# The second MLP product of a vision tower by seven quarter products instead of eight, with the sums on VectorE

## The chip, the cores and the metric

The kernel runs on one core of a Trainium2 chip. The core has TensorE (PE in the profile, with PEld for its weight loads), VectorE (DVE), ScalarE (ACT), GpSimd (POOL) and the DMA engines with their queues (SP issues most transfers here). The metric is the device time of one execution, in microseconds (us). All data is float32.

## The reference, cut to what matters

The input is cut into patches and embedded: 32 blocks of 512 tokens of width D = 256. Then comes one layer with a retention and an MLP, and then a mixture of 8 experts of which each token uses two.

```python
h = _L0_tok_ref(x, L0_tok_W)                       # patches, DFT, @ W.T
# --- retention and MLP, on layernorm(h) ---
q, k, v = h1 @ Wq.T + bq, h1 @ Wk.T + bk, h1 @ Wv.T + bv
mem = decay * mem + (k * v)_t;  ret_t = q_t * mem  # a scan over the tokens
x = x + ret
h2 = _layernorm(x, ln2_g, ln2_b)
mlp = jax.nn.relu(h2 @ W1.T + b1) @ W2.T + b2      # 256 -> 1024 -> 256
x = x + mlp
# --- mixture of experts, on layernorm(h) ---
logits = tokens @ router_w.T;  probs = softmax(logits); top 2, weights normalised
for e in range(8):
    y = gelu(tokens @ w1[e] + b1[e]) @ w2[e] + b2[e]
    out = out + combine[:, e:e + 1] * y
```

What is changed is the product `relu(...) @ W2.T`: for a block it is [512 tokens x 1024] times [1024 x 256].

## The kernel before

The main loop works on three blocks at once: `new` (block i: embedding and retention), `mid` (block i-1: MLP) and `old` (block i-2: routing). Between these parts stand `slot(known)` calls; each enters one expert tile of 256 tokens (`enter`, L799) and ends the one before (`leave`, L816, and `sums`, L833 and L835); this is 16 passes on TensorE. The order of the instructions on TensorE, VectorE, ScalarE and SP is the order of this code; each engine works through its own list. The numbers L... are line numbers of this kernel, as the profile shows them.

```python
p_mm = ...tile_pool(name="p_mm", bufs=4, space=PSUM)   # tiles "mm", 4 in turn
p_tm = ...tile_pool(name="p_tm", bufs=3, space=PSUM)   # tiles "tm", 3 in turn
p_sm = ...tile_pool(name="p_sm", bufs=1, space=PSUM)   # tile "sm", one only
...
for i in range(NS):                       # NS = 31; new, mid, old as above
    embed = new.embed(); next(embed)      # L353: 20 matmuls into three tm tiles
    if mid: mid.features2()               # hT for the MLP (L292 on ScalarE)
    if old: old.rows(); old.turn3(); old.store()     # L533: row <- tok
    next(embed); next(embed)              # L359: h of the new block, norms
    if mid: mid.sum_up()                  # L462, L463: h += z, h += b2
    next(embed, None)                     # L252: zz and z
    slot(known)
    if old: old.join3()                   # L292: tokT
    for m in range(KH):                   # KH = 8
        if mid: mid.mlp_in(m)             # L298 w1, ScalarE relu into aT (L482)
        if m == 1: new.split1()
        if m == TT - 1: slot(known)
        if m == KH - 3:
            blocks[i + 1].differences(xs.pop(i + 1))   # L330, L327
            new.features1()               # L292: hT for the retention
    if old:
        for t in range(TT): old.logits(t) # L557, into sm
    for m in range(KD):                   # KD = 2
        new.retention(m)                  # L298 wqkv; kv L418, scan L426, ret L436
        if old and m == 0: old.choose()   # L579 to L595: small sums on VectorE
    if old: take(old.i + 1, old, old.place())   # L624 into sm; L626 to L735; scatter L640
    slot(known)
    if mid: mid.mlp_out(0)                # L492, L499
    new.residual()                        # L451 transposes, L454, norm, L252 zz
    slot(known)
    ...
    new.split2()                          # zz to features2 of the next period, by DMA
    if mid: mid.mlp_out(1)                # L492, L499, norm, L252 tok
```

The part that changes:

```python
def mlp_in(self, m):
    if m == 0:
        self.aT = one.tile([P, KH, BLK], F32, name="aT")      # BLK = 512 tokens
    ps = feature_mm(w1_sb, self.hT, m)
    nc.scalar.activation(self.aT[:, m, :], ps, AF.Relu, bias=...)

def mlp_out(self, u, between=None):
    if u == 0:
        self.norm = Norm()
    ps = p_tm.tile([P, 2, D], F32, name="tm")
    for i in range(2):
        if i and between:
            between()
        for k in range(KH):
            nc.tensor.matmul(                                  # L492
                ps[:, i, :],
                lhsT=self.aT[:, k, ts(u * 2 + i, P)],          # the weights: 128 x 128 of aT
                rhs=w2_sb[:, k, :],                            # streamed: 128 x 256
                start=k == 0, stop=k == KH - 1,
            )
    nc.vector.tensor_tensor(self.h[:, ts(u, 2), :], ps, self.h[:, ts(u, 2), :], ALU.add)   # L499
    for i in range(2):
        self.norm.stats(self.h, u * 2 + i)                     # L223, L224
    if u == U - 1:
        self.norm.factors_here() if self.i >= NS - 1 else self.norm.factors()   # on POOL in the loop
        self.tok = one.tile([P, TT, D], F32, name="tok")
        self.norm.apply(self.tok, self.h)                      # L252
        ...
```

And three short pieces that the steps of the prediction use:

```python
def sums(self):                       # of an expert tile, on VectorE
    nc.vector.scalar_tensor_tensor(share, ...)                 # L828
    nc.vector.tensor_tensor(share, share, ...)                 # L831
    nc.vector.tensor_tensor(y, ps, w[...])                     # L833: reads the tile's tm
    for c in range(2):
        nc.vector.tensor_scalar(y[:, c, :], y[:, c, :], share[:, c : c + 1], None, ALU.mult)  # L835
    # then two indirect adds to out by DMA

def residual(self):
    for u in range(U):                # U = 2
        ps = p_tm.tile([P, 2, D], F32, name="tm")
        ...                           # L451: transposes of ret, 128 x 128
        nc.vector.tensor_tensor(self.z[...], ps, self.z[...], ALU.add)          # L454
        ...                           # L223, L224: statistics
    norm.factors_here()               # L231 to L237, VectorE
    norm.apply(self.zz, self.z)       # L252

# wu, once at the start, a sum of 256 elements a partition from SBUF to SBUF:
nc.vector.tensor_tensor(wu[:, 4, j, :], E_j, O_j, ALU.subtract)                 # L142
```

Of the kernel before, what the change touches and what calls it, by code (L numbers as in the profile page):

```python
# [12 lines left out]
F32 = mybir.dt.float32  # L13
I32 = mybir.dt.int32
U16 = mybir.dt.uint16
AF = mybir.ActivationFunctionType
ALU = mybir.AluOpType
AX = mybir.AxisListType

P = 128  # L20
# [15 lines left out]
def vit_tower_kernel(  # L36
# [15 lines left out]
    nc = tc.nc  # L52
    B, NBLK, _, XW = x.shape
    D = wtok.shape[2]
    C = P // 2
    H = w1.shape[1]
    E = rw.shape[1]
    KD, KH = D // P, H // P
    J = STRIDE // 2
    TT = 4  # L60
    BLK = TT * P
    U = TT // 2
# [8 lines left out]
    RW = D + 4  # L71
# [3 lines left out]
    NS = NB - 1  # L75
# [73 lines left out]
    nc.sync.dma_start(out=w1_sb, in_=w1.rearrange("(k p) h -> p k h", p=P))  # L149
    w2_sb = const.tile([P, KH, D], F32)  # L150
    nc.sync.dma_start(out=w2_sb, in_=w2.rearrange("(k p) d -> p k d", p=P))
    rw_sb = const.tile([P, KD, E], F32)
# [156 lines left out]
    class Block:  # L309
# [168 lines left out]
        def mlp_in(self, m):  # L478
# [3 lines left out]
            nc.scalar.activation(self.aT[:, m, :], ps, AF.Relu, bias=vec[:, MB1 + m : MB1 + m + 1])  # L482

        def mlp_out(self, u, between=None):
            if u == 0:
                self.norm = Norm()
            ps = p_tm.tile([P, 2, D], F32, name="tm")
            for i in range(2):
                if i and between:
                    between()  # L490
                for k in range(KH):
                    nc.tensor.matmul(  # L492
                        ps[:, i, :],
                        lhsT=self.aT[:, k, ts(u * 2 + i, P)],
                        rhs=w2_sb[:, k, :],
                        start=k == 0,
                        stop=k == KH - 1,
                    )
            nc.vector.tensor_tensor(self.h[:, ts(u, 2), :], ps, self.h[:, ts(u, 2), :], ALU.add)  # L499
            for i in range(2):  # L500
                self.norm.stats(self.h, u * 2 + i)
            if u == U - 1:
                self.norm.factors_here() if self.i >= NS - 1 else self.norm.factors()
                self.tok = one.tile([P, TT, D], F32, name="tok")
                self.norm.apply(self.tok, self.h)
                if self.i == NS:
                    nc.vector.tensor_tensor(self.h, self.h, self.tok, ALU.add)
                    return
                mean, rstd = self.norm.mv[:, :, 0], self.norm.rstd[:, 0, :]
                self.by = small.tile([P, 2, TT], F32, name="by")  # L510
                nc.vector.tensor_scalar(self.by[:, 0, :], rstd, 1.0, None, ALU.add)
                nc.vector.scalar_tensor_tensor(self.by[:, 1, :], mean, -1.0, rstd, ALU.mult, ALU.mult)

# [15 lines left out]
        def rows(self):  # L529

            self.row = two.tile([P, TT, RW], I32, name="row")
            for i, half in enumerate(halves(self.tok)):
                nc.scalar.copy(self.row.bitcast(U16)[:, :, i * D : (i + 1) * D], half)  # L533
            nc.gpsimd.iota(
                self.row[:, :, NUMBER : NUMBER + 1],
                pattern=[[1, TT]],
                base=self.i * BLK,
                channel_multiplier=TT,
            )
# [147 lines left out]
    def take(n, block, writes):  # L687
# [24 lines left out]
        shape = [1, k, E]  # L712
        past = small.tile([1, KMAX, E], F32, name="past")[:, :k, :]
        nc.vector.tensor_tensor(
# [4 lines left out]
        )  # L719
        table_f = small.tile([1, 2, KMAX], F32, name="table_f")[:, :, :k]  # L720
        nc.vector.tensor_reduce(table_f[:, 0, :], past, AX.X, ALU.add)
# [216 lines left out]
    def slot(known):  # L938

        if len(tiles) - at["enter"] > LEFT and at["enter"] + 2 <= known:  # L940
            expert_step()
# [7 lines left out]
    with tc.manual_schedule(engines=MANUAL):  # L949
        blocks[0].differences(xs.pop(0))  # L950
        xs[1] = load_x(1)
        for i in range(NS):
# [36 lines left out]
            if old:  # L989
                for t in range(TT):  # L990
                    old.logits(t)
            for m in range(KD):
                new.retention(m)
                if old and m == 0:
                    old.choose()
            if old:
                take(old.i + 1, old, old.place())
            if i + 2 < NB:
                xs[i + 2] = load_x(i + 2)
            slot(known)  # L1000
            if mid:
                mid.mlp_out(0)
            new.residual()
            slot(known)
            if at["enter"] == 0:

                advance("load", 2)
            if i == 0:
                fold(w1_sb.unsqueeze(1), G2, B2, MB1)
            else:  # L1010
                new.split2()
            if mid:
                mid.mlp_out(1)

# [27 lines left out]
        writes = old.place()  # L1042
        next(weights)
        last.retention(0)
        mid.mlp_out(0)
        next(weights)
        take(NS - 1, old, writes)
        expert_step()
        mid.mlp_out(1)
        next(weights)  # L1050
# [21 lines left out]
        for m in range(KH):  # L1072
            last.mlp_in(m)
            if m == TT - 1:
                expert_step()
        expert_step()
        last.mlp_out(0, expert_step)
        expert_step()
        last.mlp_out(1, expert_step)

# [103 lines left out]
```

## Time and profile before

| | |
|---|---|
| time, median of 3 runs | 2197.89 us (2197.12 to 2201.64) |
| span of the profiled execution | 2216.1 us |
| granted TensorE clock, mean | 0.991 |
| L492 (second MLP product), PE busy | 462.3 us, 2048 passes |
| L298 with w1 (first MLP product), PE busy | 455.4 us, 1024 passes |
| L298 with wqkv, PE busy | 342.5 us, 768 passes |
| L353 (embedding), PE busy | 284.8 us, 1280 passes |
| L499 (adding the product to h), DVE busy | 44.2 us, 64 times, 690 ns each |

The profile shows one execution. PE is the matmul row of TensorE and PEld its weight loads, which overlap it. The ends of matmuls are modelled; their starts are recorded. In a row of a group or of the timeline stand the line, the engine, the operation, the tiles written and read (out<-in), the shape (partitions x elements) and how many there are. In a group row the busy time and the mean duration follow; in the timeline the start in us comes first and then how long the row lasted; `[3.54 <-PE mm L298]` at its end is how long the engine stood idle before it and what it was waiting for. Nearly all of the span lies in the main loop, which repeats the list above 31 times.

### The profile page before, as it was taken

How to read it: one execution, taken by the hardware profiler on the slowest of the kernel's cores; microseconds unless marked ns; L12 is line 12 of the kernel's file. 1: busy time of each engine (PE TensorE's matmuls, PEld its weight loads, DVE VectorE, ACT ScalarE, POOL GpSimd, SP SyncE). 2: the span in 40 equal slices, each digit the busy share in tenths (PEclk: the TensorE clock that was granted, in tenths of full speed). 3: DMA queues.
4: the chain of work that ended last, by engine and by line, in shares of the span. 5: the costliest groups of instructions: out<-in, count | busy, mean ns of one | idle time of the engine just before them, and what ended most of it. 6: DMA issues, size and time to landing. Idle time of an engine off the chain costs nothing.

```text
span 2216.1 us, 28920 instructions
## 1 busy us (share of the span) xinstructions
PE 2161.2 (98%) x8548; PEld 1544.3 (70%) x8548; DVE 1650.9 (74%) x5150; ACT 825.6 (37%) x1329; POOL 873.1 (39%) x760
## 2 busy tenths in 40 slices
PE   8999999999999999999999999999999999998999
PEld 6666666667676667777666777666677766676676
DVE  6678877778778777877877777777787777766454
ACT  1223323444334443432444432344443334442443
POOL 0022243344444434444434444443444444344444
PEclk9999999999999999999999999999999999999999
DMA  3022265676565677657567656665765666588743
GB/s 135 20 97 75 79 147 125 134 163 122 127 149 135 143 139 150 125 129 155 129 139 149 135 128 135 149 136 132 163 130 130 138 146 137 115 172 205 116 66 45
DMA packets 425389, 284.95 MB, mean 129 GB/s; under 512 B 355216, under 2 KB 391056, under 8 KB 421136
## 3 DMA queue, kind: packets, MB, share of 16 engines
q1 hardware_dynamic: 374304, 210.21, 41.4%
q0 software_dynamic: 49632, 67.39, 16.1%
q10 hardware_dynamic: 1296, 5.52, 1.0%
q8 instruction: 67, 1.10, 0.2%
q14 instruction: 90, 0.74, 0.1%
HBM read 118.36 MB, written 88.39 MB: 93 GB/s over the span
## 4 chain that ended last, share of the span: by engine, by line
PE 88%; DVE 3%; DMA 3%; ACT 3%; issue 2%; another core or an unknown queue 0%; POOL 0%; ACTq 0%; DVEq 0%; SPq 0%; POOLq 0%
PE mm L298 31%; PE tm L492 19%; PE tm L353 11%; PE mm L799 9%; PE tm L816 9%; DMA turned<-planes 3%; PE sm L557 2%; PE tm L888 1%; PE tm L451 1%; PE mm L871 1%; PE mm L131 1%; PE mm L265 1%; ACT h L518 1%; ACT row L533 1%; ACT hT L292 1%
## 5 line engine op out<-in xcount | busy, mean ns | idle before, releaser
L839 POOL DMA_INDIRECT out<-y,xg x262 | 429.3, 1638 | 501.0 <-DVE y L835 225.9
L492 PE MATMUL tm<-w_sb,aT 128*128 128x256 f32 x2048 | 462.3, 380 | 16.5 <-issue 14.6
L298 PE MATMUL mm<-hT,w_sb 128*128 128x512 f32 x1024 | 455.4, 596 | 10.7 <-ACT ge L807 5.7
L492 PEld LDWEIGHTS tm<-w_sb,aT 128*128 128x128 f32 x2048 | 387.2, 190 | 80.8 <-issue 27.1
L298 PEld LDWEIGHTS mm<-hT,w_sb 128*128 128x128 f32 x1024 | 193.9, 191 | 232.6 <-issue 207.6
L298 PE MATMUL mm<-hT,wqkv_sb 128*128 128x512 f32 x768 | 342.5, 602 | 4.2 <-DVE hT L292 4.2
L640 POOL DMA_INDIRECT xbuf<-row,to x248 | 242.3, 977 | 258.8 <-DVE full L699 182.4
L807 ACT ACTIVATE ge<-mm,w 128x256 f32<-128x256 f32 x262 | 109.3, 469 | 574.3 <-issue 525.8
L353 PE MATMUL tm<-wu,xv 128*128 128x256 f32 x1280 | 284.8, 381 | 0.0
L298 PEld LDWEIGHTS mm<-hT,wqkv_sb 128*128 128x128 f32 x768 | 145.3, 192 | 176.4 <-issue 160.4
L353 PEld LDWEIGHTS tm<-wu,xv 128*128 128x128 f32 x1280 | 244.3, 191 | 33.3
L799 PE MATMUL mm<-xT,w 128*128 128x256 f32 x1048 | 251.3, 383 | 1.5 <-DVE tile_share L828 1.5
L816 PE MATMUL tm<-w,ge 128*128 128x256 f32 x1048 | 247.6, 379 | 0.9 <-DVE y L833 0.9
L482 ACT ACTIVATE aT<-mm,vec 128x512 f32<-128x512 f32 x256 | 169.9, 684 | 173.7 <-PE mm L298 170.5
L799 PEld LDWEIGHTS mm<-xT,w 128*128 128x128 f32 x1048 | 195.6, 191 | 38.6 <-issue 13.1
L816 PEld LDWEIGHTS tm<-w,ge 128*128 128x128 f32 x1048 | 199.0, 190 | 31.3 <-issue 3.4
L792 ACT COPY xT<-xh 128x512 uint16<-128x512 uint16 x262 | 181.2, 761 | 5.4 <-DMA xh<-xbuf 5.3
L243 POOL TENSOR_SCALAR rstd<-mv 128x4 f32<-128x4 f32 x62 | 41.6, 671 | 319.2 <-DVE mv L224 317.3
L833 DVE TENSOR_TENSOR y<-tm,w 128x512 f32<-128x512 f32 x131 | 90.6, 692 | 70.5 <-PE tm L816 69.7
L416 ACT ACTIVATE ks<-mm,vec 128x512 f32<-128x512 f32 x64 | 44.0, 687 | 248.6 <-PE mm L298 248.6
L597 POOL TENSOR_TENSOR ex<-euler,second 128x4 f32<-128x4 f32 x32 | 34.7, 1084 | 247.1 <-DVE second L589 247.1
L418 DVE SCALAR_TENSOR_TENSOR kv<-mm,vec,ks 128x512 f32<-128x512 f32 x64 | 47.9, 748 | 108.9 <-PE mm L298 108.9
(155 smaller groups left out, 2498.2 us busy)
## 6 DMA issues: line engine op xcount, KB each, us to landing
w<-in_wex SPq DMA_DIRECT2D x113, 641.5 KB
xb<-in_x SPq DMA_DIRECT2D x32, 1040.0 KB
out<-h SPq DMA_DIRECT2D x31, 512.0 KB
bank<-in_wex ACTq DMA_DIRECT2D x8, 641.5 KB
out<-y,xg POOLq DMA_INDIRECT x262
xbuf<-row,to POOLq DMA_INDIRECT x248
xh<-xbuf SPq DMA_TRANSPOSE x131
xg<-xbuf SPq DMA_DIRECT2D x131, 4.0 KB
```

Source lines behind the costliest of these rows:

```text
L298: nc.tensor.matmul(ps, lhsT=w[:, k, ts(m, P)], rhs=rhs[:, k, :], start=k == 0, stop=k == KD - 1)
L353: nc.tensor.matmul(ps[:, n, :], lhsT=xv[:, i, j, :], rhs=wu[:, i, j, :], start=j == 0, stop=j == J - 1)
L418: nc.vector.scalar_tensor_tensor(own_order(self.kv[:, m, :]), tiles_order(pv), vec[:, BV + m : BV + m + 1], own_order(ks), ALU.add, ALU.mult,)
L482: nc.scalar.activation(self.aT[:, m, :], ps, AF.Relu, bias=vec[:, MB1 + m : MB1 + m + 1])
L492: nc.tensor.matmul(ps[:, i, :], lhsT=self.aT[:, k, ts(u * 2 + i, P)], rhs=w2_sb[:, k, :], start=k == 0, stop=k == KH - 1,)
L640: write = nc.gpsimd.indirect_dma_start(out=xbuf, out_offset=bass.IndirectOffsetOnAxis(ap=to[:, c, t : t + 1], axis=0), in_=self.row[:, t, ...
L792: nc.scalar.copy(halves[:, :, :, 1 - i], self.xh[:, i * KD : (i + 1) * KD, :])
L799: nc.tensor.matmul(ps[:, m, :], lhsT=self.w[:, k * D + m * P : k * D + (m + 1) * P], rhs=self.xT[:, k, :], start=k == 0, stop=k == KD - 1,)
L807: nc.scalar.activation(self.ge[:, m, :], ps[:, m, :], AF.Gelu, bias=self.w[:, 5 * D + m : 5 * D + m + 1])
L816: nc.tensor.matmul(ps[:, c, :], lhsT=self.ge[:, k, ts(c, P)], rhs=w[:, (2 + k) * D : (3 + k) * D], start=k == 0, stop=k == KD - 1,)
L833: nc.vector.tensor_tensor(y, ps, w[:, 4 * D : 5 * D].unsqueeze(1).to_broadcast([P, 2, D]), ALU.add)
L839: add = nc.gpsimd.indirect_dma_start(out=out, out_offset=bass.IndirectOffsetOnAxis(ap=self.xg[:, c, NUMBER - D : NUMBER - D + 1], axis=0), ...
```

## The change: Strassen's scheme for one product

The activations aT of a block (512 tokens x 1024) are cut into four quarters, A11 and A12 (tokens 0 to 255; the first and second half of the 1024), A21 and A22 (tokens 256 to 511), and W2 into B11, B12, B21, B22 (the halves of the 1024 and of the 256 output columns). The plain product needs eight products of quarters; the form used here (Strassen's, as arranged by Winograd) needs seven, with sums of quarters before and sums of products after. It is meant to take work from TensorE.

- Four weight sums T1 to T4 are formed once, on VectorE.
- For each block VectorE forms S1 = A21 + A22, S2 = S1 - A11, S3 = A11 - A21 (in place of A21) and S4 = A12 - S2. They lie in the buffers named tok, tokT, aT and kv.
- A product of quarters is 8 matmuls with 128 x 128 of the activations as weights and 128 x 128 of W2 streamed, where before 128 x 256 were streamed.
- `mlp_out` has three parts in place of two. Part 0 multiplies A11 B11 into one half of an sm tile, and ScalarE copies it to U, which takes the place of a part of A11. Part 1 multiplies A12 B21 and A22 T4. Part 2 multiplies S2 T2, S1 T1, S3 T3 and S4 B22. VectorE adds the products to U and to h.
- To make room, the buffer `row` has one copy instead of two, and so have two tables of `take`.

The diff, cut to its core:

```diff
-    w2_sb = const.tile([P, KH, D], F32)
-    nc.sync.dma_start(out=w2_sb, in_=w2.rearrange("(k p) d -> p k d", p=P))
+    w2_sb = const.tile([P, 7, KQ, P], F32)          # KQ = 4
+    w2_raw = w2.rearrange("(r k p) (c d) -> p r c k d", p=P, k=KQ, d=P)
+    for i, (r, c) in {B11: (0, 0), B21: (1, 0), B22: (1, 1), T1: (0, 1)}.items():
+        nc.sync.dma_start(out=w2_sb[:, i], in_=w2_raw[:, r, c])
+    def combine_weights():
+        ...                                         # T3, T1, T2, T4: four sums on VectorE
...
+        def combine1(self):
+            ...                                     # A11, A12, A21, A22: views of aT
+            self.S1 = one.tile(shape, F32, name="tok")       # shape = [P, KQ, 256]
+            self.S2 = one.tile(shape, F32, name="tokT")
+            self.S3 = self.A21
+            nc.vector.tensor_tensor(self.S1, self.A21, self.A22, ALU.add)
+            nc.vector.tensor_tensor(self.S2, self.S1, self.A11, ALU.subtract)
+            nc.vector.tensor_tensor(self.S3, self.A11, self.A21, ALU.subtract)
+        def combine2(self, place):
+            self.S4 = one.tile([P, KQ, BLK // 2], F32, name=place)
+            nc.vector.tensor_tensor(self.S4, self.A12, self.S2, ALU.subtract)
         def mlp_out(self, u, between=None):
-            ...                                     # as shown above
+            def product(to, a, b):
+                for i in range(2):
+                    for k in range(KQ):
+                        nc.tensor.matmul(to[:, i, :], lhsT=a[:, k, ts(i, P)],
+                                         rhs=w2_sb[:, b, k, :], start=k == 0, stop=k == KQ - 1)
+            def add(to, what):
+                nc.vector.tensor_tensor(to, to, what, ALU.add)
+            h = self.h.rearrange("p (a i) (c d) -> p a c i d", i=2, d=P)
+            U = self.aT[:, 0, : BLK // 2].rearrange("p (i d) -> p i d", d=P)
             if u == 0:
+                self.ps = p_sm.tile([P, 2, 2, P], F32, name="sm")
+                product(self.ps[:, 0], self.A11, B11)
+                nc.scalar.copy(U, self.ps[:, 0])
+                add(h[:, 0, 0], U)
+                return
+            if u == 1:
+                ps = p_tm.tile([P, 2, 2, P], F32, name="tm")
+                product(ps[:, 0], self.A12, B21)
+                if between:
+                    between()
+                product(ps[:, 1], self.A22, T4)
+                add(h[:, :, 0], ps)
+                return
+            product(self.ps[:, 1], self.S2, T2)
+            add(U, self.ps[:, 1])
+            add(h[:, 0, 1], U)
+            product(self.ps[:, 0], self.S1, T1)
+            add(h[:, :, 1], self.ps[:, 0].unsqueeze(1).to_broadcast([P, 2, 2, P]))
+            if between:
+                between()
+            ps = p_tm.tile([P, 2, 2, P], F32, name="tm")
+            product(ps[:, 0], self.S3, T3)
+            add(U, ps[:, 0])
+            add(h[:, 1], U.unsqueeze(1).to_broadcast([P, 2, 2, P]))
+            product(ps[:, 1], self.S4, B22)
+            add(h[:, 0, 1], ps[:, 1])
+            self.norm = Norm()
+            for t in (2, 3, 0, 1):
+                self.norm.stats(self.h, t)
...
-            self.row = two.tile([P, TT, RW], I32, name="row")
+            self.row = one.tile([P, TT, RW], I32, name="row")
... in the main loop:
+            if mid:
+                mid.combine1()                      # after the logits, before the retention
             for m in range(KD):
                 new.retention(m)
...
             if old:
                 take(old.i + 1, old, old.place())
+            if mid:
+                mid.combine2("kv")
...
             slot(known)
             if mid:
                 mid.mlp_out(0)
             new.residual()
+            if mid:
+                mid.mlp_out(1)
             slot(known)
...
             if i == 0:
                 fold(w1_sb.unsqueeze(1), G2, B2, MB1)
+                combine_weights()
             else:
                 new.split2()
             if mid:
-                mid.mlp_out(1)
+                mid.mlp_out(2)
... (the last two blocks, after the loop, in the same manner)
```

## The prediction

> **What bounds the kernel now.** I read the page first, then the chain that ended last, then the groups of instructions by shape, and last the timeline of one period of the main loop, engine by engine. From the page:
>
> ```profile
> PE 2161.2 (98%) x8548; PEld 1544.3 (70%) x8548; DVE 1650.9 (74%) x5150; ACT 825.6 (37%) x1329; POOL 873.1 (39%) x760
> ...
> PE 88%; DVE 3%; DMA 3%; ACT 3%; issue 2%; another core or an unknown queue 0%; POOL 0%; ACTq 0%; DVEq 0%; SPq 0%; POOLq 0%
> ```
>
> TensorE is the bound: 98% busy, and 88% of the chain is its own work. VectorE (DVE) has 26% to spare on the average. The embedding's first matmul (L353) starts at 329.6 us for one block and at 1955.0 us 25 blocks later, so a period lasts 65.0 us. I take the one from 1501.13 to 1566.13 us. Its windows show TensorE busy 63.78 and VectorE 50.56 of the 65.00; the part from 1537.46 to 1552.55 has VectorE busy 13.60 of 15.09. So its slack is not spread evenly. The timeline of the weight loads and matmuls in this period:
>
> ```profile
> 1531.96 1.75 PEld L557 LDWEIGHTS sm<-rw_sb,tokT 128*128 128x128 f32 x15 [0.24 <-issue]
> ...
> 1544.41 1.97 PE L799 MATMUL mm<-xT,w 128*128 128x256 f32 x8
> 1546.22 1.89 PE L816 MATMUL tm<-w,ge 128*128 128x256 f32 x8
> 1547.94 7.07 PE L492 MATMUL tm<-w_sb,aT 128*128 128x256 f32 x32
> 1554.85 1.04 PE L451 MATMUL tm<-ident,ret 128*128 128x128 f32 x8
> 1555.72 1.89 PE L799 MATMUL mm<-xT,w 128*128 128x256 f32 x8
> ```
>
> Each written f32 matmul appears twice (32 rows for the 16 of one `mlp_out(u)`): two passes. Sixteen passes of an expert tile run from 1544.41 to 1547.94. Passes of width 256 follow each other at (7.07-0.38)/31 = 0.216 us (0.38 is the length of one). And of VectorE:
>
> ```profile
> 1525.29 0.69 DVE L833 TENSOR_TENSOR y<-tm,w 128x512 f32<-128x512 f32 x1 [1.09 <-PE tm L816]
> ...
> 1532.46 1.46 DVE L292 COPY hT<-turned 128x512 uint16<-128x512 uint16 x4
> 1537.46 0.75 DVE L418 SCALAR_TENSOR_TENSOR kv<-mm,vec,ks 128x512 f32<-128x512 f32 x1 [3.54 <-PE mm L298]
> ...
> 1552.84 0.69 DVE L833 TENSOR_TENSOR y<-tm,w 128x512 f32<-128x512 f32 x1
> ...
> 1555.05 0.69 DVE L499 TENSOR_TENSOR h<-tm,h 128x512 f32<-128x512 f32 x1 [0.87 <-PE tm L492]
> ...
> 1563.27 1.39 DVE L252 TENSOR_SCALAR zz<-z,mv,rstd 128x256 f32<-128x256 f32 x4
> ```
>
> The reader is to see how little VectorE waits from 1525.29 on: 3.54 us before `kv` and 0.87 us before L499, in 39 us. L833 frees the PSUM tile that the next user of its `tm` buffer needs, at 1553.53; the transposes, which come after the 6.9 us of `mlp_out(0)`, need it at about 1555. That is a margin of 1.5 us and no more.
>
> [...] L142 419, L330 683, L462 1193 and L463 1225 ns. [...] loads alone (L557) come every (1.75-0.19)/14 = 0.111 us, and the 128-wide transposes (L451) every (1.04-0.27)/7 = 0.110 us. [...] The trace before has no tile of which one half is read while the other is written[...]; but the changed program does order such pairs by semaphores.
>
> **The change part by part.**
>
> *TensorE.* Before: 64 passes a block x 0.216 = 13.8 us. After: 7 products x 8 matmuls x 2 passes = 112 passes of width 128. At 0.112 us (the load's pace, which the stream of 128 just matches) that is 12.5 us. Saved 1.3 us a block, some 42 us in 32 blocks, 1.9%. That is all there is to win: 1/8 of 13.8 is 1.7, and the per-pass overhead takes part of it.
>
> *VectorE.* Added a block: three sums of 1024 (`combine1`) 3 x 1.22 = 3.7; one more (`combine2`) 1.22; `h`+=`U` (256) 0.45; a sum of 512 from PSUM 0.72; in `mlp_out(2)` four of 256 and two of 512, 4 x 0.42 + 2 x 0.70 = 3.1. Removed two of 512, 1.4. Net about 8 us, so that 50.6 becomes about 58.5 us a period; the waits in the stretch shown above are 4.4 us in all. ScalarE gets one small copy, which I take as hidden.
>
> *Waits.* Where TensorE used to have `mlp_out(0)` of 6.9 us between the third expert tile and the transposes, it now has one product of 1.8. I measure t from the start of a period (1501.13 before).
>
> 1. VectorE's run from L833 of the second tile (t = 22.8 after, set by TensorE: 8.63 embedding, two tiles of 3.45, 6.87 of MLP input, then latency). To the end of the hT copies: 8.63 (1525.29 to 1533.92). `combine1`: 3.7; it falls into the 3.54 us wait, so it is nearly free. From `kv` to the end of L735: 15.09 (1537.46 to 1552.55). `combine2`: 1.22. Tile shares and L833: 1.06. That makes t = 52.5.
> 2. `mlp_out(1)` takes the `tm` buffer of the third tile, so it waits for that L833. TensorE is there early: t = 22.6 + 6.87 + 1.75 logits + 10.3 retention + 0.4 + 3.5 tile + 1.8 product + 0.9 transposes = 48.1. **First stall: about 4.4 us.**
> 3. VectorE goes on: L835 0.65, `h`+=`U` 0.45, residual with norm and zz 7.8 (1556.86 to 1564.66), the 512 sum 0.7, the fourth tile's sums 1.7, `U`+= second product 0.45: t = 64.2.
> 4. TensorE after the stall: `mlp_out(1)` 3.6, tile 3.5, product S2 T2 1.8: ready at t = 61.4. The next product goes into the other half of the same `sm` tile, and the changed program makes it wait for `U`+=. **Second stall: about 2.8 us.** The product S4 B22 waits in the same way for `U`+= of S3 T3: about 0.65 us more.
> 5. From t = 64.2 TensorE still has 3 x 1.79 + 0.65 = 6.0, so the period ends at t = 70.2.
>
> Period 70.2 against 65.0: +5.2 us, which is the stalls of 7.85, less the 1.3 saved and less the 1.2 us of waits that TensorE had before (65.00 - 63.78) and that fall into the new ones. There are 26 such periods (expert tiles present from 265.1 us on): +135. The four earlier periods with an MLP have no tiles between, so TensorE waits longer, at `sm` for `place` and then for `U`: by the same addition +3, +6, +9, +9, in all +27. Two blocks at the end, +6; forming the weight sums at the start, four of 512 on VectorE, +2. Sum: 2198 + 170 = **2368 us**; I say 2365.
>
> **The rivals.** (A) *The products decide.* If VectorE kept up, 2198 - 42 = about 2156 us. For it: 26% of VectorE idle on average and `combine1` fitting its gap. Against it: the chain of step 1 to 3 is 41.5 us long without a wait. (B) *VectorE alone is the bound*, TensorE hiding behind it: a period of at least the 58.5 us of VectorE's work, which is less than TensorE's, so no loss. This is why averages mislead: the two engines take turns. (C) *The narrow matmul is slow*: if loads and streams did not overlap, a pass would take 0.111 + 0.109 = 0.22 us and a block 24.6 us, +11 a period; part of that hides in the stalls (of 112 passes, 48 lie after the last one), so some +5 us a period on top of mine, near 2500 us. The transposes, spaced by 0.110 with a load each, speak against it. (D) *A single `row` buffer* makes the copy wait for the last scatter; in the period shown the last scatter (L640) is issued by 1559.8, 6.3 us before the period ends, and the copy (L533) comes 12.7 us into a period (1513.85), so I give it nothing.
>
> **Range and chances.** The stalls are differences of long sums; an error of 1.5 us a period moves the time by 40 us, and the early periods by 10 more. With half of all the stalls (loop and early periods) the same sum gives about 2255, still over 2%. Range 2300 to 2420. Faster by over 2% would need more than rival A gives; within 2%, less than half of the stalls.
>
> **What would show it.** The L353 starts should be about 70 us apart. The 128-wide passes should be spaced by 0.11 us. TensorE's waits should name DVE: the y sum of the expert tile before `mlp_out(1)`, and `aT` (`U`) inside `mlp_out(2)`, at some 4 and 3 us each. VectorE should be about 83% busy and TensorE about 90%. Wrong if these waits are absent, or if `mlp_out` passes are spaced by over 0.13 us.

## The result and the profile after

The changed kernel takes **2388.09 us** (2386.07 to 2388.66) against 2198.14 us (2197.12 to 2201.64) for the kernel before: ratio 1.0859, 95% interval 1.0841 to 1.0878. It is slower by 190 us; 2365 was predicted, with a range of 2300 to 2420.

In the kernel after, L366 is the embedding, L311 the first MLP product and the retention, L520 the seven products, L505 to L507 `combine1`, L511 `combine2`, L529 the adds of products to `h` and U, L860 and L877 an expert tile, L894 its y sum, L464 the transposes. Its page, busy time and chain:

```profile
PE 2199.6 (92%) x10084; PEld 1627.6 (68%) x10084; DVE 1878.2 (79%) x5474; ACT 843.7 (35%) x1361; POOL 914.1 (38%) x760
...
PE 54%; DVE 40%; issue 3%; DMA 1%; POOL 1%; DVEq 0%; ACT 0%; SPq 0%; POOLq 0%; ACTq 0%
```

TensorE's share of the chain has fallen from 88% to 54% and VectorE's has risen from 3% to 40%, though neither engine is busier than 92%. The two engines wait for each other: VectorE for TensorE 63.6 us before L894 (54 times) and 60.5 us before the add of the product in sm (32 times). The waits of TensorE (line waited for: us in all, times, longest):

```profile
PE tm L520 <- DVE y L894: 104.7, 26, 4.4
PE sm L520 <- DVE aT L529: 32.9, 32, 5.0
PE tm L520 <- DVE aT L529: 16.9, 32, 1.0
PE sm L520 <- DVE before L691: 11.4, 4, 3.7
```

The first is the stall before `mlp_out(1)`: 26 periods at 4.0 us. The second and third stand inside `mlp_out(2)`; the last belongs to the four early periods. TensorE's timeline in one period, from the end of the third expert tile on:

```profile
1612.52 1.89 PE L877 MATMUL tm<-w,ge 128*128 128x256 f32 x8
1614.37 2.02 PE L520 MATMUL sm<-w_sb,aT 128*128 128x128 f32 x16
1616.22 1.04 PE L464 MATMUL tm<-ident,ret 128*128 128x128 f32 x8
1621.29 5.18 PE L520 MATMUL tm<-w_sb,aT 128*128 128x128 f32 x32 [4.03 <-DVE y L894]
...
1629.76 1.95 PE L520 MATMUL sm<-w_sb,tokT 128*128 128x128 f32 x16
1632.58 2.05 PE L520 MATMUL sm<-w_sb,tok 128*128 128x128 f32 x16 [0.87 <-DVE aT L529]
1634.47 1.95 PE L520 MATMUL tm<-w_sb,aT 128*128 128x128 f32 x16
1636.93 2.05 PE L520 MATMUL tm<-w_sb,kv 128*128 128x128 f32 x16 [0.51 <-DVE aT L529]
```

The three stalls of the prediction are there, at 4.03, 0.87 and 0.51 us. And of VectorE in the same period:

```profile
1602.57 1.22 DVE L507 TENSOR_TENSOR aT<-aT 128x1024 f32<-128x1024 f32 x1
1603.76 0.75 DVE L431 SCALAR_TENSOR_TENSOR kv<-mm,vec,ks 128x512 f32<-128x512 f32 x1
...
1619.06 1.21 DVE L511 TENSOR_TENSOR kv<-aT,tokT 128x1024 f32<-128x1024 f32 x1
...
1620.54 0.69 DVE L894 TENSOR_TENSOR y<-tm,w 128x512 f32<-128x512 f32 x1
```

`combine1` ends at 1603.79 and `kv` follows with no wait: the 3.54 us gap of the kernel before is filled. `combine2` stands in the run that leads to L894, whose start at 1620.54 and length give 1621.23; TensorE resumes at 1621.29.

One thing was not predicted: 32 passes of `mlp_out(1)` take 5.18 us where the same 32 would take 3.6. The windows over the stall, the 3.41 us after it and the rest of the period (us, busy time of PE, PEld, DVE, ACT, POOL, then PEclk, DMA share and GB/s):

```profile
1617.26:1621.29 4.03, 0.00 (x2) 0.00 (x1) 3.75 (x16) 0.86 (x2) 3.23 (x3) 0.93 0.47 98
1621.29:1624.70 3.41, 3.41 (x18) 3.41 (x19) 3.27 (x10) 0.00 (x0) 2.68 (x3) 0.58 0.71 273
1624.70:1639.04 14.34, 12.96 (x98) 12.14 (x98) 9.49 (x32) 2.83 (x4) 8.81 (x8) 1.00 0.75 149
```

After the idle 4.03 us the granted clock is 0.58 in the mean of 3.4 us, then full again: the starts of the first 14 passes lie 213 ns apart for the most part, 2.9 us in all, and those of the others 112.

### The profile page after: what moved, and what is told of

Read it like the earlier page. It is cut to its first block, busy times and chain, and to the rows that moved or that the text cites. A ratio compares the mean times of both kernels' runs of the same rounds, so it can differ in the third digit from the quotient of the medians.

```text
span 2386.0 us, 32582 instructions
## 1 busy us (share of the span) xinstructions
PE 2199.6 (92%) x10084; PEld 1627.6 (68%) x10084; DVE 1878.2 (79%) x5474; ACT 843.7 (35%) x1361; POOL 914.1 (38%) x760
## 4 chain that ended last, share of the span: by engine, by line
PE 54%; DVE 40%; issue 3%; DMA 1%; POOL 1%; DVEq 0%; ACT 0%; SPq 0%; POOLq 0%; ACTq 0%
PE mm L311 12%; PE tm L366 12%; PE tm L520 9%; PE mm L860 6%; PE tm L877 6%; PE sm L520 4%; DVE xv L343 3%; DVE ks L439 3%; DVE xv L340 3%; DVE ret L449 3%; DVE y L894 2%; DVE kv L431 2%; DVE hT L305 1%; DVE tokT L506 1%; DVE y L896 1%
## 5 line engine op out<-in xcount | busy, mean ns | idle before, releaser
L900 POOL DMA_INDIRECT out<-y,xg x262 | 435.3, 1662 | 474.3 <-DVE y L896 151.9
L311 PE MATMUL mm<-hT,w_sb 128*128 128x512 f32 x1024 | 452.0, 594 | 0.2 <-ACT hT L279 0.2
L701 POOL DMA_INDIRECT xbuf<-row,to x248 | 275.4, 1111 | 258.6 <-DVE full L760 181.8
L311 PEld LDWEIGHTS mm<-hT,w_sb 128*128 128x128 f32 x1024 | 194.6, 191 | 218.0 <-issue 212.5
L311 PE MATMUL mm<-hT,wqkv_sb 128*128 128x512 f32 x768 | 338.8, 597 | 0.0
L520 PE MATMUL tm<-w_sb,aT 128*128 128x128 f32 x1536 | 241.4, 329 | 104.7 <-DVE y L894 104.7
L520 PEld LDWEIGHTS tm<-w_sb,aT 128*128 128x128 f32 x1536 | 233.8, 243 | 111.0 <-DVE y L894 110.8
L366 PE MATMUL tm<-wu,xv 128*128 128x256 f32 x1280 | 284.5, 381 | 0.0
L366 PEld LDWEIGHTS tm<-wu,xv 128*128 128x128 f32 x1280 | 241.8, 191 | 31.7
L311 PEld LDWEIGHTS mm<-hT,wqkv_sb 128*128 128x128 f32 x768 | 144.0, 191 | 169.3 <-issue 154.7
L860 PE MATMUL mm<-xT,w 128*128 128x256 f32 x1048 | 251.5, 383 | 1.7 <-DVE tile_share L889 1.4
L877 PE MATMUL tm<-w,ge 128*128 128x256 f32 x1048 | 248.1, 380 | 0.9 <-ACT ge L868 0.9
L860 PEld LDWEIGHTS mm<-xT,w 128*128 128x128 f32 x1048 | 195.0, 191 | 38.8 <-issue 15.7
L877 PEld LDWEIGHTS tm<-w,ge 128*128 128x128 f32 x1048 | 199.5, 190 | 31.6 <-issue 3.4
L375 ACT COPY ab<-tm 128x512 f32<-128x512 f32 x32 | 18.8, 587 | 374.9 <-PE tm L366 374.9
L894 DVE TENSOR_TENSOR y<-tm,w 128x512 f32<-128x512 f32 x131 | 90.6, 692 | 64.1 <-PE tm L877 63.6
```

The source lines that it names most:

```text
L311: nc.tensor.matmul(ps, lhsT=w[:, k, ts(m, P)], rhs=rhs[:, k, :], start=k == 0, stop=k == KD - 1)
L366: nc.tensor.matmul(ps[:, n, :], lhsT=xv[:, i, j, :], rhs=wu[:, i, j, :], start=j == 0, stop=j == J - 1)
L520: nc.tensor.matmul(to[:, i, :], lhsT=a[:, k, ts(i, P)], rhs=w2_sb[:, b, k, :], start=k == 0, stop=k == KQ - 1,)
L701: write = nc.gpsimd.indirect_dma_start(out=xbuf, out_offset=bass.IndirectOffsetOnAxis(ap=to[:, c, t : t + 1], axis=0), in_=self.row[:, t, ...
L860: nc.tensor.matmul(ps[:, m, :], lhsT=self.w[:, k * D + m * P : k * D + (m + 1) * P], rhs=self.xT[:, k, :], start=k == 0, stop=k == KD - 1,)
L877: nc.tensor.matmul(ps[:, c, :], lhsT=self.ge[:, k, ts(c, P)], rhs=w[:, (2 + k) * D : (3 + k) * D], start=k == 0, stop=k == KD - 1,)
```

## The experiments

Each kernel was timed with the kernel before beside it on the same chip, so each is read by its ratio to that. They did not all run on one chip. **Theory of turns**: TensorE and VectorE each wait for the other inside the block, because products share tiles and VectorE's sums stand between them. **Rivals**: VectorE's total work is the bound; or the narrow passes themselves are slow.

### Move the first wait

```diff
             if u == 1:
-                ps = p_tm.tile([P, 2, 2, P], F32, name="tm")
+                ps = p_mm.tile([P, 2, 2, P], F32, name="mm")
```

> The tile of mlp_out(1) comes from the pool of four (mm) instead of the pool of three (tm), so it no longer waits for the y sum (L894) of the third expert tile; nothing else changes. Theory of the chain (a period is VectorE's unbroken run from the second tile's y sum to U += second product, 41.4 us, plus what TensorE has left, 28.8 us): the wait of 4 us before mlp_out(1) goes, but the wait inside mlp_out(2) grows from 0.9 to about 7 us, and because TensorE's half clock after the idle time now falls on products that lie behind the last wait, the period gets 0 to 1.6 us longer: 2390 to 2430 us. Rival (each wait costs its own length): 26 x 4.0 = 104 us less, about 2285 us.

Measured 2432.6 us against 2209.2, ratio 1.1008 (1.0989 to 1.1026). The wait for L894 has gone, and the wait for U has grown from 32.9 to:

```profile
PE sm L520 <- DVE aT L529: 187.4, 32, 6.5
```

VectorE sets when U is ready, so taking away one wait only lengthened the next. That each wait costs its own length is refuted. The product behind the longer wait is then slower, in one period:

```profile
1659.15 3.78 PE L520 MATMUL sm<-w_sb,tok 128*128 128x128 f32 x16 [6.51 <-DVE aT L529]
```

In the changed kernel it takes 2.05 us. The granted clock of a whole execution is 0.951 here and 0.961 there.

### Leave out the sums

One kernel leaves out the three sums of `combine1` (S1, S2 and S3 are the quarters themselves), another the one sum of `combine2` (S4 is A12). Neither computes the reference's MLP.

```diff
-            ...                                   # the tiles of S1, S2 and S3
-            nc.vector.tensor_tensor(self.S1, self.A21, self.A22, ALU.add)
-            nc.vector.tensor_tensor(self.S2, self.S1, self.A11, ALU.subtract)
-            nc.vector.tensor_tensor(self.S3, self.A11, self.A21, ALU.subtract)
+            self.S1, self.S2, self.S3 = self.A21, self.A22, self.A21
```

> combine1 is left out: the products take quarters of aT as they are, so the output is not the reference's. 3.66 us less VectorE work a block. Theory of the chain: combine1 fills the time in which VectorE would wait for the retention's second product, so only some 0.2 us a period comes back: 2378 to 2388 us. Rival (VectorE's total work sets the time): 32 x 3.66 = 117 us less, about 2271 us.

Measured 2413.3 us, ratio 1.0919 (1.0900 to 1.0937). Its waits:

```profile
PE tm L515 <- DVE y L889: 104.4, 26, 4.0
...
DVE kv L431 <- PE mm L311: 108.5, 32, 5.8
```

VectorE has 3.7 us a period less to do, waits 108.5 us for `kv` instead (2.9 in the changed kernel), and the stall stays 104.4. The time did not fall at all. The sums of `combine1` are free, and VectorE's total work is not the bound.

```diff
-            self.S4 = one.tile([P, KQ, BLK // 2], F32, name=place)
-            nc.vector.tensor_tensor(self.S4, self.A12, self.S2, ALU.subtract)
+            self.S4 = self.A12
```

> combine2 is left out (the last product takes A12 as it is), 1.22 us less VectorE work a block, a third of what the run without combine1 leaves out. Theory of the chain: it stands in the part without any wait, so it comes back in full: 30 x 1.22 = 37 us less, about 2351 us (2345 to 2358). Rival (the sums are hidden, the cost lies in the narrow passes or in the handing over): no change, 2388 us.

Measured 2438.5 us, ratio 1.1044 (1.1023 to 1.1065): the expectation failed. The first stall did shrink, from 104.7 to 75.3 us (1.1 us in each of 26 periods, the length of the sum), but two new waits came:

```profile
PE tm L519 <- DVE y L893: 75.3, 26, 2.9
...
PE sm L519 <- issue: 35.0, 54, 1.8
...
DVE h L528 <- remote: 55.8, 25, 2.9
```

"remote" and "issue" are waits whose cause the profile does not name. They became the second question of this study. The "issue" waits cut the product S2 T2 into pieces, and the two products behind it were then slower, in one period:

```profile
1515.46 3.78 PE L519 MATMUL sm<-w_sb,tok 128*128 128x128 f32 x16 [1.56 <-DVE aT L528]
1519.03 3.11 PE L519 MATMUL tm<-w_sb,aT 128*128 128x128 f32 x16
```

They take 2.05 and 1.95 us in the changed kernel. So what the shorter first stall gave was lost again behind it.

### Narrow passes alone

The kernel before, with each matmul of 256 columns made as two of 128. Nothing is left out.

```diff
-                for k in range(KH):
-                    nc.tensor.matmul(ps[:, i, :], lhsT=..., rhs=w2_sb[:, k, :], ...)
+                for c in range(2):
+                    for k in range(KH):
+                        nc.tensor.matmul(ps[:, i, ts(c, P)], lhsT=..., rhs=w2_sb[:, k, ts(c, P)], ...)
```

> The kernel before, with each 256-wide matmul of the second MLP product made as two of 128 columns: 128 passes a block instead of 64, and no sums on VectorE. It measures the narrow pass alone. Theory: 0.112 us a pass, 128 x 0.112 = 14.3 us a block against 13.8, so 16 us more in 32 blocks: about 2214 us. Rival (load and stream do not overlap, 0.22 us a pass): 14 us more a block, about 2650 us.

Measured 2425.2 us, ratio 1.0974 (1.0956 to 1.0992), far from the 2214 us expected, but not for the rival's reason. TensorE's timeline, and below it the add that reads the product:

```profile
1557.77 7.31 PE L493 MATMUL tm<-w_sb,aT 128*128 128x128 f32 x64
1564.91 1.04 PE L451 MATMUL tm<-ident,ret 128*128 128x128 f32 x8
1565.79 1.89 PE L800 MATMUL mm<-xT,w 128*128 128x256 f32 x8
1574.55 3.75 PE L817 MATMUL tm<-w,ge 128*128 128x256 f32 x8 [6.88 <-DVE h L500]
```

```profile
1573.72 0.69 DVE L500 TENSOR_TENSOR h<-tm,h 128x512 f32<-128x512 f32 x1 [9.60 <-remote]
```

The 64 passes are (7.31-0.27)/63 = 0.112 us apart (0.27 is the length of one), so narrow passes run at the predicted pace. By the modelled end the product is done at 1565.08, but the add starts 8.6 us later; the profile puts the wait down to "remote". The add waits in this way 26 times (235.1 us in all), as many as there are periods with expert tiles.

### The changed kernel once more, the products alone, and a tile for each product

> The changed kernel unaltered, on the chip of this call, as the base of the other two. The first four experiments ran on a chip on which the kernel before took 2209 us instead of 2198, and all four showed a stretch in each period in which the engines that wait for TensorE start up to 9 us after the product ended; the profile of the changed kernel on the first chip showed none. If that lateness belongs to the chip, this run shows none on the first chip (2388 us) and shows it on the other (2400 to 2415 us). If it belongs to the program, none is seen here on any chip.

Measured 2402.9 us against 2205.8, ratio 1.0899 (1.0881 to 1.0917). I counted in the traces how many of TensorE's recorded completions came more than 0.6 us after the modelled end of the matmul. Where some completions are missing from the record, the count depends on which matmul each is put down to, and the least possible is given: 60 of 1267 here, none in the first profile of the same program, 97 of 1160 in that of the kernel before. So lateness comes and goes with the chip or the run, and here it moves the ratio by 0.4% at most: it is not what made the change slow.

The products alone leave out the sums S1 to S4, the copy to U and all but two adds, and `mlp_out(1)` writes an mm tile, as in the first experiment:

```diff
-            add(U, self.ps[:, 1])
-            add(h[:, 0, 1], U)
             product(self.ps[:, 0], self.S1, T1)
-            add(h[:, :, 1], self.ps[:, 0].unsqueeze(1).to_broadcast([P, 2, 2, P]))
             ...                                   # S3 T3, S4 B22 in one tm tile
+            add(h[:, :, 1], ps)
```

> The seven products alone: no sums S1 to S4 before them, no adds to U; the only reads are two adds of 512 elements a partition to h, one for each tile, and mlp_out(1) writes a tile of the mm pool, so that it waits for no expert sum. It computes something else than the MLP. Theory of turns (VectorE's work between the products is what costs): nothing stands between the products any longer, and with 56 narrow passes where 64 wide ones were, TensorE has about 2.4 us a period less to do than before: period about 62.6 us, total about 2155 us. Rival (narrow passes and the second set of weight loads cost time by themselves, whoever reads the product): still above the kernel before, about 2300 us or more.

Measured 2341.3 us, ratio 1.0620 (1.0603 to 1.0638): the number is in the rival's range, but the trace shows neither theory. TensorE's timeline in the third part, in pieces:

```profile
1515.91 0.40 PE L514 MATMUL sm<-w_sb,aT 128*128 128x128 f32 x2 [1.03 <-issue]
1517.45 0.35 PE L514 MATMUL sm<-w_sb,aT 128*128 128x128 f32 x1 [1.15 <-issue]
1519.11 3.60 PE L514 MATMUL sm<-w_sb,aT 128*128 128x128 f32 x16 [1.31 <-issue]
```

Here TensorE itself halts: one or two matmuls at a time, with gaps of 1.0 to 1.3 us, waiting for nothing that the profile shows. The last 16 passes take 3.60 us, where A11 B11, of 16 passes too, takes 2.02 us in the same period. This comes at the end of a stretch in which its completions are late by up to 8.6 us (a GELU starts at 1519.30, and the product it reads ends at 1510.67).

The other kernel keeps everything and gives each product a tile of its own (the pair in `mlp_out(1)`, which one add reads, keeps one tile, and that add moves behind the expert tile's sums):

```diff
-                self.ps = p_sm.tile([P, 2, 2, P], F32, name="sm")     # A11 B11, in mm now
+            p2 = p_mm.tile([P, 2, P], F32, name="mm")                 # S2 T2
+            p1 = p_mm.tile([P, 2, P], F32, name="mm")                 # S1 T1
+            add(h[:, :, 0], self.ps)      # of mlp_out(1), now after the expert tile's sums
             ...
+            p3 = p_tm.tile([P, 2, P], F32, name="tm")                 # S3 T3
+            p4 = p_tm.tile([P, 2, P], F32, name="tm")                 # S4 B22
```

> All sums and adds stay, the result is the same; but each product has a tile of its own (A11 B11, the pair A12 B21 and A22 T4, S2 T2 and S1 T1 in mm tiles, S3 T3 and S4 B22 in a tm tile each), and the add after mlp_out(1) stands behind the sums of the expert tile. So TensorE never waits for VectorE within the product. Theory of turns: the three stalls go (5 us a period), and VectorE's list (57.5 us of work in a period of 70.4) then fits beside TensorE: period about 65 to 66 us, total 2200 to 2260 us, close to the kernel before. Rival (VectorE's total work is the bound, whatever the turns): the waits move to the next place where TensorE needs VectorE, and the time stays within 1% of the changed kernel, 2365 to 2410 us.

Measured **2241.6 us**, ratio 1.0173 (1.0142 to 1.0203). The same products and sums take 161 us less than the changed kernel beside it, and the granted clock is 0.991 instead of 0.962. The largest waits of TensorE are now:

```profile
PE mm L311 <- ACT ge L871: 27.1, 24, 1.2
PE tm L520 <- issue: 17.7, 53, 0.9
```

No wait for VectorE within the product is left. This settles the main question: most of the loss (9.0% became 1.7%) was the turns, made by shared tiles, with the slower passes behind the stalls; it was neither VectorE's work nor the narrow passes.

### What makes completions late

In the traces with late completions the stretch begins when the 641 KB of an expert tile's weights arrive while GpSimd's scatter of rows is going on; that load is issued in the third slot of the period. In the products alone it is issued at 1507.28 us, beside a scatter that starts at 1504.54, and the product that ends at 1508.94 is the first that is late. The next kernels issue the loads of the third and fourth slot after `mlp_out(2)` instead.

```diff
-            slot(known)                     # third slot; the fourth in the same way
+            slot(known, load=False)
...
             if mid:
                 mid.mlp_out(2)
+            if at["enter"]:
+                advance("load", at["enter"] + AHEAD - 1)
```

First, on the products alone (which leave out the same sums and adds as before):

> The seven products alone took 2341 us where 2155 were expected. In its trace the matmuls of S2 T2, in the third part, start one or two at a time, 1.0 to 1.3 us apart, for some 5 us of each period, and the engines that wait for TensorE in the 9 us before it start late. In each period the 641 KB of weights of an expert tile come in then, issued in the third slot, while GpSimd scatters the rows. This kernel is the same (sums and most adds left out), but the loads of the third and fourth slot are issued after mlp_out(2). Theory (the load that runs beside the scatter holds TensorE's completions up): the gaps of 1.0 to 1.3 us within the product and the late starts go, and the time falls to 2155 to 2210 us. Rival (the scatter does it alone, or the narrow passes themselves): the gaps stay where the scatter is, and the time stays within 1% of 2341 us.

Measured 2215.9 us, ratio 1.0054 (1.0028 to 1.0080), where the same kernel with early loads had 1.0620. Not one completion is late (82 of 1167 before, at the least), and the product that came in pieces now runs through, together with the next:

```profile
1562.18 3.73 PE L514 MATMUL sm<-w_sb,aT 128*128 128x128 f32 x32
```

The time lies just above the expected range, and still above the kernel before: TensorE now waits 22.4 us (25 times) for hT. The narrow passes are the same in both kernels, so they did not cost the 6%.

Second, on the kernel with a tile for each product, nothing left out:

> The kernel with a tile for each product (2241.6 us), with the loads of the third and fourth slot issued after mlp_out(2), nothing left out. Theory (the load beside the scatter holds completions up, and it also slows the transposing DMAs of features2, which stand in this kernel's chain of waits for 8.6% of its span): TensorE's pauses without a visible wait in the last product (17.7 us in all) go and hT comes earlier: 2205 to 2230 us. Rival: the same time within 0.5%, as VectorE's list (84% of the span) sets the period.

Measured 2260.8 us, ratio 1.0271 (1.0244 to 1.0297): slower, not faster. Again no completion is late, and the pauses named "issue" are gone, but TensorE waits 57.9 us (25 times, 2.3 each) for VectorE's copy of hT. VectorE's largest waits are for GpSimd's rstd, 70.8 us in all before `tok` and 59.4 before `zz` (2.29 and 1.84 in one period), and 50.0 us (27 times) for the retention's product. Why this was worse than with the early loads stays open.

Third, with ScalarE's row copies ahead of hT of the MLP and its scaling of h (for the store) after the first MLP product; nothing left out:

> As the one before, and ScalarE takes the rows of the routed block before hT of the MLP and scales h for its store after the first MLP product instead of before the first slot, so that the GELU of the first slot comes 2 us earlier and the transposed rows reach VectorE earlier. Nothing is left out. If the waits of TensorE for ScalarE's GELU (24 times 1.1 us) and the wait of VectorE for the turned rows are on the path, 25 to 40 us go: 2175 to 2205 us, at or a little under the kernel before on this chip (2206 us). If VectorE's list alone sets the period: no more than 0.5% better than the kernel with late loads.

Measured 2225.4 us, ratio 1.0126 (1.0090 to 1.0161): better by 1.4%, but not under the kernel before and not in the expected range. TensorE's wait for the GELU, which this was to remove, had been 27.1 us with the early loads and was only 0.3 us with the late ones. Its wait for VectorE's hT fell from 57.9 to 12.9 us, and one for ScalarE's hT, now behind the rows, came in its place (28.5 us in 24 waits).

### Filling VectorE's two waits, with seven and with eight products

Both kernels have the late loads and these moves, and leave nothing out:

```diff
             if mid:
                 mid.features2()
+            next(embed)                     # the embedding's first adds, before tok
             if old:
+                old.finish()                # tok and by, cut from the end of mlp_out
                 old.rows()
                 old.turn3()
-                old.store()                 # now after the first MLP product
             ...
-            next(embed, None)
             slot(known)
+            next(embed, None)               # zz and z, after the first slot
```

> The seven products with a tile each and the late loads (2260.8 us), and three moves that fill VectorE's waits; nothing is left out. In that kernel VectorE's list is without a gap but for two waits for GpSimd's rstd in each period (2.29 us before tok, 1.84 us before zz), and TensorE waits 2.2 us for hT. Here tok is formed after the embedding's first adds, the first slot comes before zz, and the scaling of h for its store stands after the first MLP product. Theory (VectorE's list with its two waits sets the period once the turns are gone): 4.1 us of each period go, TensorE's 62.6 us of work become the bound, and the time is 2145 to 2185 us, under the kernel before (2204 us). Rival (the latency of the transposing DMAs from zz to hT sets the period): TensorE's wait for hT stays at about 2 us and the time at 2215 us or more.

> The kernel before, with eight products, and the same moves: late loads, tok after the embedding's first adds, the first slot before zz, the scaling of h later. Nothing is left out. It tells what the seven products bring when all else is alike. If TensorE bounds both kernels then, this one is behind the seven products by what they save, about 2.4 us a period or 60 to 75 us: 2195 to 2225 us, about as the kernel before, which has little to gain from VectorE. If the moves themselves are the gain, this one is as fast as the other.

Measured: seven products **2153.6 us**, ratio 0.9789 (0.9760 to 0.9819); eight products 2173.3 us, ratio 0.9868 (0.9847 to 0.9889). Both beat the kernel before. The windows of one period of each, seven first:

```profile
1521.50:1583.60 62.10, 62.10 (x302) 45.93 (x300) 57.31 (x171) 26.04 (x43) 29.62 (x25) 1.00 0.64 145
```

```profile
1538.90:1602.30 63.40, 63.40 (x253) 45.62 (x252) 50.93 (x161) 25.82 (x42) 27.81 (x23) 1.00 0.63 142
```

Both windows show TensorE busy from end to end, at full clock; they are among the shortest periods of the two runs. In them the seven products save 63.40 - 62.10 = 1.30 us, and VectorE does 57.31 us of work beside them instead of 50.93. In the mean of the 26 periods with expert tiles a period takes 62.8 us against 63.7, so 0.9 is saved: with seven products, more periods still hold a wait. In all they save 19.8 us, and the slowest run with seven (2163.5) is under the fastest with eight (2169.4). The moves and the late loads together save 26.8 (2200.1 to 2173.3) without them, which is the larger part; the two were not tried apart. The eight products were expected at 2195 to 2225 us, and my 60 to 75 us between the two was wrong: I had taken 65.0 - 62.6 for the saving of the products, and that difference also held the 1.2 us of waits of the kernel before.

## Why the prediction was right, step by step

It was right in direction and size, and most steps within a period held closely (t counts from the embedding's first matmul, at 1569.0 in the period shown):

| step | predicted | measured |
|---|---|---|
| passes of 128 columns | 0.112 us apart | 0.112 at full clock (half of a pass of 256: 0.108) |
| VectorE's sums of 256, 512, 1024 | 0.42 to 0.45, 0.70 to 0.72, 1.22 us | 0.42, 0.68 to 0.69, 1.21 to 1.23 us |
| `combine1` | nearly free | `kv` waits 2.9 us in all, 108.9 before |
| start of the first stall | t = 48.1 | 48.3 |
| first stall | 4.4 us | 4.0 |
| second stall | 2.8 us | 0.9 |
| third | 0.65 us | 0.5 |
| period | 70.2 us | 69.8 in the one shown, 70.4 in the mean of 26 |
| TensorE, VectorE busy | 90%, 83% | 92%, 82% in the one shown |

- **Step 4, the second stall, was mis-sized.** It counted `mlp_out(1)` as 3.6 us. After the first stall the granted clock was 0.58 in the mean of 3.4 us, and the next matmul started 5.0 us after it (1621.29 to 1626.30). From the end of the first stall TensorE took 10.4 us to the second instead of 8.9, and VectorE, which ends that wait, 11.2 instead of 11.7. So the slower passes used up about 1.5 us that would have been waiting, and the period hardly changed. In the first experiment they lay behind the last long wait: there 16 passes took 3.78 us instead of 2.05, and the period was 71.8 us in the mean of 26 instead of 70.4, on another chip.
- **The other terms.** The 26 periods gave +140.4 us where +135 was predicted. The four early periods: +3, +6, +9, +9 predicted (27), and +4.3, +10.0, +9.1, +11.4 measured (34.8). The tail gave -5 instead of +6, the start nothing instead of +2. That these errors cancel, so that the sum agrees to 0.1 us, is luck.
- **The base was taken wrongly.** From one profiled span to the other the sum is 2386.0 - 2216.1 = 169.9 us, and +170 was predicted. But the period of 65.0 us was read from the profiled execution of the kernel before, whose span is 18 us over its median, and the sum was added to the median. These are 18 of the 23 us by which 2365 fell short; 3 more went when 2368 was rounded to 2365, and 2 lie between the span and the time of the changed kernel. What made that execution longer is not shown. It held pauses of TensorE in L492 and a late completion:

```profile
PE tm L492 <- issue: 14.6, 34, 1.0
DVE h L499 <- remote: 9.0, 2, 8.6
```

The wait of 8.6 us ends at 2018.5 us, in the tail of the kernel before, where +6 was predicted and -5 measured.
- **Rivals.** A (2156 us) assumed that VectorE keeps up; in the rearranged kernel it nearly does. Its term, 1.3 us saved a block, is confirmed by 63.40 against 62.10 for a period in which TensorE never stops. That 2153.6 us was measured there is luck: of the 46.5 us under the kernel before, 26.8 come from the moves and the late loads, and the products give 19.8, not 42. B was refuted by leaving out `combine1`; its remark that the two take turns is what the separate tiles showed. C was refuted by the pace of the passes, 0.112 us; its 0.109 us for a stream of 128 was an estimate, near half of the 0.216 us of a pass of 256. D: the copy into `row` waits 1.4 us in all, for `tok`, and no engine has a large wait for the scatter.

## What to carry to other kernels

Before giving an engine with idle time more work, follow one period along its instruction list and find where the other engine must wait for it: a share of 74% did not show how little margin TensorE had at one place (1554.85 - 1553.53 = 1.3 us by the lines of the prediction, which says 1.5). Give each product that another engine reads a tile of its own, so that it can run on (here 9.0% became 1.7%), and fill the waits the profile shows with work that is ready. Only then did a saving of 0.9 us in 63 appear in the time, and the waits filled on the way brought more than the products. And a time read from a profiled execution belongs to that execution's span, not to the median.

## What had not been expected of the hardware

- **Half clock after a stall of 4 us.** Around the end of the idle 4.03 us, from 1620.73 to 1624.14 us, the granted clock was 0.50, and the passes were 213 ns apart for 2.9 us, against 112 behind them. After 2.90 us idle (the kernel without `combine2`), 32 passes took 3.84 us, (3.84-0.27)/31 = 0.115 us apart. In the products alone the idle time came in pieces: between gaps of 1.03, 1.15 and 1.31 us TensorE was busy for 0.40 and 0.35 us, and the 16 passes after that took 3.60 us. What decides it is not shown.
- **Completions of TensorE that came more than 8 us late.** The add of the narrow-pass kernel came 8.6 us after the modelled end of its product. What held it up in between is not shown. Of the nine profiles with the load of weights beside the scatter, eight had late completions, at least 14 to 116 of them, and one (the first of the changed kernel) none; of the five with the loads moved, none had any. The kernel pairs that differ in this alone ran on different chips. So that moving the load cures it is strongly suggested, above all by 1.0054 against 1.0620, and not proven; a kernel with the scatter moved instead wasn't tried.
- **What a late completion costs depends on who waits.** In the changed kernel it was 0.4% at most (1.0899 against 1.0859). In the narrow-pass kernel the next expert tile needed the late add, and TensorE waited for it 168.5 us in all, 26 times, 6.5 us each.
